# Query and key projections of three head groups by seven products instead of eight, with the output-side query blocks moved and the weight-transform levels rescheduled

## The chip, the cores and the metric

The kernel runs on one core of a Trainium2 chip. The metric is the time of one execution on the device, in microseconds (us). A core has a matrix engine (TensorE, PE in the profile, with its weight loads as PEld), VectorE (DVE), ScalarE (ACT), GpSimd (POOL) and SyncE (SP), which in this kernel only issues DMAs. Each engine takes its instructions in program order and stops at one whose inputs are not ready; everything queued behind it on that engine stops too. The engines wait for each other by semaphores.

## The reference

The input is one sequence `x` of 2048 tokens with 256 features, in float32, and everything is computed in float32. There are two layers, each a layer norm, the layer, another layer norm and the addition to the residual. The first is differential attention, the second a small feed-forward network whose inputs and hidden values pass through a Walsh-Hadamard transform (`fwht`).

```python
x = x + layernorm(attention(layernorm(x)))
x = x + layernorm(ffn(layernorm(x)))

def attention(x):                       # 8 query pairs, 4 key/value groups, D = 128
    q, k, v = split(x @ Wqkv.T + b)     # q: 8 pairs of 2 heads; k: 4 pairs; v: 4 of 256 columns
    p1 = causal_softmax(q[:, 0] @ k[:, 0].T * D ** -0.5)
    p2 = causal_softmax(q[:, 1] @ k[:, 1].T * D ** -0.5)
    o = (p1 - lam * p2) @ v             # 2048 x 256 for each query pair
    o = o * rsqrt(mean(o * o) + eps) * subln_w * (1 - LAMBDA_INIT)
    return concat(o) @ out_w.T + out_b

def ffn(x):                             # 256 -> 1024 -> 256
    x = fwht(x * SU_ug) / 64
    h = silu(x @ W_gate.T * s_gate) * (x @ W_up.T * s_up)
    return (fwht(h * SU_dp) / 64) @ W_down.T * s_down
```

## The kernel before

**Groups and units.** The attention is done for one key/value group `g` (0 to 3) after the other. A group has two query pairs and one key pair, so its projection for 512 tokens (a token block `nb`, 0 to 3) has four parts: the query pairs `j2` = 0 and 1, the key pair `j2` = 2 (256 output columns each, as two heads of 128) and the 256 value columns (part 3). `load_qkv` brings the group's weights `wq`. The attention itself is cut into 96 units, 24 per group. A unit is one tile `i` of 128 tokens, with both of its 64-token halves for `i` below 8 (128 rows here are 64 tokens times two query pairs) and with one half for `i` from 8 on. Group 0 goes through its units with growing `i`; groups 1 to 3 begin with the longest, `i` = 15, and end with `i` = 0. Thus group g begins at unit 24g, the long units of steps 24g to 24g+15 are followed by the short ones, and the last step before a new group has the least attention work.

**Steps.** One loop runs over the steps 0 to 102 and issues, at each, pieces of several units, each piece to the queues of its engines; nothing but this order decides what runs when. The unit of this step gets its scores, the previous one (`mixed`) its combination and its way through DRAM, the one of three steps ago (`ripe`, LAG = 3) its product with the values; `out1` to `out4` are one to four steps older than `ripe`. The order within a step is:

1. the functions in `before[step]`
2. `scores(new, 0)`: TensorE makes scores into PSUM, VectorE moves them to SBUF (`e`) with a row minimum. `exponentials(new, 0)` on ScalarE
3. `inverse(out1)`: GpSimd scales an attention output by its inverse norm. `accumulate(out4)`: VectorE adds an output projection to `acc`. `turn_out(out2)`: VectorE transposes a scaled output, SyncE sends it to DRAM
4. `combine(mixed)`: VectorE forms `p1 - lam * p2`. `move`: VectorE transposes it, SyncE sends it to DRAM (`dr`) and fetches it back as `pt` in four DMAs. For some short units, among them those of groups 1 and 2, the move is issued later, after step 6 of this list
5. the functions in `mid[step]` and then in `between[step]`
6. `pad` (a GpSimd memset), `scores(new, 1)`
7. `values(ripe)`: TensorE multiplies `pt` with the values; ScalarE copies the sum out and takes its squares. `project_out(out3)`: TensorE multiplies with the output weights
8. `exponentials(new, 1)`, then the functions in `after[step]`

`put(where, step, f, ...)` hangs a function into one of the dictionaries `before`, `mid`, `between` and `after`; `put_block` does so for the parts of a token block's projection.

**PSUM.** The pool `ps_s` has three tiles of 128 x 1024, tag `sc`, which scores, all projections and the feed-forward products use in turn; `ps_o` has two tiles for the value products and output projections. A TensorE instruction that is to write a tile waits until the reader of its last contents is done.

**Projections.** `project_heads(g, nb, j2)` makes two heads for 512 tokens: for each head `h` two matmuls of 512 columns (`c` = 0, 1 over the 256 features) into one half of a PSUM tile. A float32 matmul leaves two records in the trace. The first half goes to `qT` or `kT` by a ScalarE activation (L200), the other by a VectorE operation (L202), both with scale (`-SCALE` for queries) and bias. `project_values` makes the values of a block with 8 matmuls of 256 columns. In group 1 the key blocks and block 3's queries are in `before[24]`, the other query blocks in `between` of steps 25 to 30. For groups 2 and 3, beginning at step `end` = 48 and 72, blocks 3, 2 and 1 are in `between` of steps `end`-5 to `end`-1, and block 0 follows, its queries in `between` of `end` and `end`+1.

**Feed-forward weights.** Rather than transform the activations, the kernel transforms the weights. For each of `up`, `gate` and `down`, in a pool `tmp` with two tags `t0` and `t1` of 128 x 2048: `load_weights` (a GpSimd-issued DMA into `t0`, named `raw_...`), for `down` a scaling on ScalarE (`scale_down`), the levels of the transform (`transform(which, n)`, eight GpSimd additions and subtractions of 128 x 256 each, going from one tag to the other; 8 levels for `up` and `gate`, 10 for `down`), `turn_weights` (four VectorE transposes of the result into a tile `x_...` of the tag `t1`, the fourth followed by a SyncE DMA to DRAM, `dw_...`). In before, the levels of `up` are hung into steps 7 to 14, `gate` 18 to 23, `down` 28 to 35, and the pool closes after step 40. From step 74 on the weights are fetched from DRAM (`arrive_weights`).

**The end.** From step 92 on the feed-forward network follows, in pieces between the last units, and after them.

Of the kernel before, what the change touches and what calls it, by code (L numbers as in the profile page):

```python
# [10 lines left out]
F32 = mybir.dt.float32  # L11
BF16 = mybir.dt.bfloat16
AF = mybir.ActivationFunctionType
ALU = mybir.AluOpType
# [35 lines left out]
def kernel(  # L50
# [64 lines left out]
    with ExitStack() as actx:  # L115
# [55 lines left out]
        def project_heads(g, nb, j2, both=True, n=512):  # L171

            wq = loaded[g][0]
            cols4 = ts(nb, n)
            xb, lo = divmod(nb * n, 512)
            nt = n // P
            pp = ps_s.tile([P, 1024], F32, tag="sc", name=f"pp_{g}_{nb}_{j2}_{n}")
            for h in range(2):
                j = 2 * j2 + h
                for c in range(2):  # L180
                    nc.tensor.matmul(  # L181
                        pp[:, 512 * h : 512 * h + n],
                        lhsT=wq[:, c, ts(j, P)],
                        rhs=xnT[:, xb, c, lo : lo + n],
                        start=(c == 0),
                        stop=(c == 1),
                    )
            for h in range(2):
                j = 2 * j2 + h
                col = g * 4 + j if j < 4 else H + g * 2 + j - 4  # L190
                bias = colv[:, C_QKB + col : C_QKB + col + 1]
                src = pp[:, 512 * h : 512 * h + n]
                if j < 4:
                    dst = qT[h][:, ts(nb, nt), :, j2, :].rearrange("d t s q -> d (t s) q")
                    src = src.rearrange("d (t q) -> d t q", q=64)
                else:
                    dst = kT[h][:, cols4]
                scale = -SCALE if j < 4 else 1.0
                if h == 0 or not both:
                    nc.scalar.activation(dst, src, AF.Identity, bias=bias, scale=scale)  # L200
                else:
                    nc.vector.tensor_scalar(dst, src, scale, bias, ALU.mult, ALU.add)  # L202

        def project_values(g, nb):

# [597 lines left out]
        place = {(u.g, u.i, u.subs[0]): k for k, u in enumerate(units)}  # L803


        before, mid, between, after = {}, {}, {}, {}

        def put(where, step, f, *args, **kw):
            where.setdefault(step, []).append(lambda: f(*args, **kw))
# [1 line left out]
        def put_block(where, steps, g, nb, parts, both=True):  # L811
            for step, part in zip(steps, parts):
                if part == 3:
                    put(where, step, project_values, g, nb)
                else:
                    put(where, step, project_heads, g, nb, part, both=both)


        put(before, 0, warm_up)
# [98 lines left out]
        for step in range(len(units) + LAG + 4):  # L918
# [16 lines left out]
                combine(mixed)  # L935
            moved = out2 if complete(out2) else None

            late = mixed and mixed.ns == 2 and (0 < mixed.g < NG - 1 or mixed.g == 0 and mixed.i in (3, 4))
            if not late:
                move(mixed, moved)  # L940
            for f in mid.get(step, ()):
                f()
# [5 lines left out]
            if new:  # L948
                pad(new)
                scores(new, 1)  # L950
            if late:
# [76 lines left out]
```

## Time and profile before

| | |
|---|---|
| median of 3 executions | 1439.21 us (1438.75 to 1439.45) |
| the profiled execution | 1438.5 us, span 1436.7 us, granted TensorE clock 0.999 |
| busy: PE, PEld | 1429.4 (99%), 1042.5 (73%) |
| busy: DVE, ACT, POOL | 976.7 (68%), 503.8 (35%), 362.3 (25%) |
| PE by line | po L376 488.0, sc L268 477.6, pp L181 170.7, pout L443 120.9 |
| POOL, transform L603, all three weights | 163.1 |
| stretch 200 to 400, 400 to 600 | DVE 133.8, 146.2; POOL 68.6, 88.8 |
| stretch 600 to 800, 800 to 1000 | DVE 121.5, 119.5; POOL 24.2, 25.3 |

The span is the time from the first to the last recorded instruction of one profiled execution; the execution takes 1.8 us more than its span. All times within the run are counted from the span's start. "L181" is line 181 of the kernel. The rows give a line, an engine, an operation, the tile it writes and the tile it reads; a count follows an x. The stretches show how VectorE's and GpSimd's work is spread over the run; TensorE is busy for all of each.

### The profile page before, as it was taken

How to read it: one execution, taken by the hardware profiler on the slowest of the kernel's cores; microseconds unless marked ns; L12 is line 12 of the kernel's file. 1: busy time of each engine (PE TensorE's matmuls, PEld its weight loads, DVE VectorE, ACT ScalarE, POOL GpSimd, SP SyncE). 2: the span in 40 equal slices, each digit the busy share in tenths (PEclk: the TensorE clock that was granted, in tenths of full speed). 3: DMA queues.
4: the chain of work that ended last, by engine and by line, in shares of the span. 5: the costliest groups of instructions: out<-in, count | busy, mean ns of one | idle time of the engine just before them, and what ended most of it. 6: DMA issues, size and time to landing. Idle time of an engine off the chain costs nothing.

```text
span 1436.7 us, 16896 instructions
## 1 busy us (share of the span) xinstructions
PE 1429.4 (99%) x5436; PEld 1042.5 (73%) x5436; DVE 976.7 (68%) x1789; ACT 503.8 (35%) x1114; POOL 362.3 (25%) x684
## 2 busy tenths in 40 slices
PE   9999999999999999999999999999999999999998
PEld 7567777656766777776677776676777777888887
DVE  6588787847556777544867678445776788656774
ACT  3453433323133334323433334323424445531111
POOL 2037725830028821011111111111111121121110
PEclk9999999999999999999999999999999999999999
DMA  5379899856667897832798887631999999732110
GB/s 147 74 176 201 190 183 222 175 89 139 154 135 145 166 208 179 165 86 62 156 184 178 172 199 168 129 81 52 208 204 192 193 196 188 173 91 81 52 56 18
DMA packets 501433, 210.76 MB, mean 147 GB/s; under 512 B 396032, under 2 KB 499456, under 8 KB 501216
## 3 DMA queue, kind: packets, MB, share of 16 engines
q1 hardware_dynamic: 498128, 200.73, 66.1%
q0 software_dynamic: 2352, 8.26, 2.1%
q8 instruction: 44, 0.72, 0.2%
q10 hardware_dynamic: 864, 0.68, 0.2%
q14 instruction: 45, 0.37, 0.1%
HBM read 111.05 MB, written 98.57 MB: 146 GB/s over the span
## 4 chain that ended last, share of the span: by engine, by line
PE 99%; DMA 0%; DVE 0%; POOL 0%; issue 0%; ACT 0%; POOLq 0%; DVEq 0%
PE po L376 33%; PE sc L268 32%; PE pp L181 11%; PE gu L706 8%; PE pout L443 8%; PE pd L741 4%; PE pv L210 4%; DMA vb<-in_vbias 0%; PE warm L479 0%; DVE v L217 0%; PE pst L508 0%; ACT q L200 0%; POOL lt L536 0%; DVE stx L90 0%; POOL rsx L95 0%
## 5 line engine op out<-in xcount | busy, mean ns | idle before, releaser
L376 PE MATMUL po<-v,pt 128*128 128x256 f32 x2176 | 488.0, 379 | 0.0
L268 PE MATMUL sc<-k,q 128*128 128x512 f32 (+11 forms) x1280 | 477.6, 519 | 0.3 <-DVE last L281 0.2
L376 PEld LDWEIGHTS po<-v,pt 128*128 128x128 f32 x2176 | 426.5, 196 | 66.5 <-issue 18.3
L268 PEld LDWEIGHTS sc<-k,q 128*128 128x128 f32 x1280 | 240.7, 190 | 200.1 <-issue 156.7
L293 ACT ACTIVATE e<-e,last 128x192 f32<-128x192 f32 (+28 forms) x256 | 298.9, 1169 | 199.4 <-DVE last L281 181.8
L286 DVE TENSOR_SCALAR_CACHE_REDUCE e<-sc 128x1024 f32<-128x1024 f32 (+1 forms) x128 | 149.2, 1166 | 153.3 <-PE sc L268 153.3
L389 ACT COPY osb<-po 128x256 f32<-128x256 f32 (+1 forms) x96 | 42.6, 443 | 483.4 <-PE po L376 482.5
L403 POOL TENSOR_TENSOR u<-ss,ed 128x1 f32<-128x1 f32 (+1 forms) x96 | 20.0, 208 | 750.1 <-ACT po L392 749.9
L325 DVE SCALAR_TENSOR_TENSOR e<-e,cf,e 128x64 f32<-128x64 f32 (+31 forms) x128 | 174.1, 1381 | 3.4
L345 DVE STREAM_TRANSPOSE e<-e 128x1536 f32<-128x1536 f32 (+7 forms) x96 | 166.6, 1735 | 7.1
L181 PE MATMUL pp<-xnT,wq 128*128 128x512 f32 (+1 forms) x408 | 170.7, 568 | 0.1
L281 DVE CUSTOM_DVE_ANT_0 e<-sc,mask 128x64 f32<-128x64 f32 (+15 forms) x128 | 89.2, 718 | 79.9 <-PE sc L268 78.7
L181 PEld LDWEIGHTS pp<-xnT,wq 128*128 128x128 f32 x408 | 77.0, 190 | 79.2 <-issue 76.1
L281 DVE CUSTOM_DVE_ANT_0 e<-sc,mask,mx 128x384 f32<-128x384 f32 (+13 forms) x128 | 105.7, 826 | 23.8 <-PE sc L268 8.4
L443 PE MATMUL pout<-wo,oT 128*128 128x256 f32 x512 | 120.9, 379 | 0.0
L443 PEld LDWEIGHTS pout<-wo,oT 128*128 128x128 f32 x512 | 97.3, 190 | 12.8
L719 ACT ACTIVATE hT<-gu,colv 128x256 f32<-128x256 f32 x64 | 26.8, 470 | 120.9 <-PE gu L706 120.8
L706 PE MATMUL gu<-fxnT,wgate 128*128 128x256 f32 x256 | 65.8, 379 | 0.0
L706 PE MATMUL gu<-fxnT,wup 128*128 128x256 f32 x256 | 65.7, 379 | 0.0
L406 POOL TENSOR_SCALAR osb<-osb,f 128x256 f32<-128x256 f32 x128 | 62.5, 488 | 11.9
L404 POOL TENSOR_TENSOR f<-u,mhalf 128x1 f32<-128x1 f32 (+1 forms) x96 | 58.3, 608 | 7.5
L725 DVE SCALAR_TENSOR_TENSOR hT<-gu,colv,hT 128x256 f32<-128x256 f32 x64 | 30.6, 478 | 41.0 <-ACT hT L719 41.0
(100 smaller groups left out, 1079.5 us busy)
## 6 DMA issues: line engine op xcount, KB each, us to landing
dr<-e SPq DMA_DIRECT2D x20, 1024.0 KB, 4.7
pt<-dr SPq DMA_DIRECT2D x80, 256.0 KB, 5.7
dr<-e SPq DMA_DIRECT2D x20, 896.0 KB, 4.5
pt<-dr SPq DMA_DIRECT2D x80, 224.0 KB, 5.1
do<-xo SPq DMA_DIRECT2D x64, 256.0 KB, 3.8
oT<-do SPq DMA_DIRECT2D x256, 64.0 KB, 2.6
dr<-e SPq DMA_DIRECT2D x20, 768.0 KB, 4.3
pt<-dr SPq DMA_DIRECT2D x80, 192.0 KB, 4.5
```

The source lines that it names most:

```text
L181: nc.tensor.matmul(pp[:, 512 * h : 512 * h + n], lhsT=wq[:, c, ts(j, P)], rhs=xnT[:, xb, c, lo : lo + n], start=(c == 0), stop=(c == 1),)
L268: nc.tensor.matmul(src[:, k, :], lhsT=qT[m][:, u.i, u.subs[a]].rearrange("d p q -> d (p q)"), rhs=kT[m][:, lo : lo + w // n], start=True, ...
L281: nc.vector.tensor_tensor_reduce(dst, src, msk, 1.0, best, ALU.add, ALU.min, accum_out=u.last[:, k0 : k0 + 1])
L286: nc.vector.tensor_scalar(dst, src, 1.0, best, ALU.mult, ALU.min, accum_out=least)
L293: nc.scalar.activation(e, e, AF.Exp, bias=u.last[:, 2 * a + m : 2 * a + m + 1], scale=-1.0, accum_out=u.d[:, a, m : m + 1],)
L325: nc.vector.scalar_tensor_tensor(e0, e1, cf[:, a : a + 1], e0, ALU.mult, ALU.add)
L345: nc.vector.transpose(x[:, : 256 * ng].rearrange("p (g c r) -> p r g c", g=ng, r=2), e[:, : 256 * ng].rearrange(order, g=ng, r=2),)
L376: nc.tensor.matmul(u.po[:, ts(a, HID)], lhsT=ptv[:, g, r, :], rhs=vt[:, kc, :], start=(kc == 0), stop=(kc == u.i),)
L404: nc.gpsimd.tensor_tensor(f[:, : u.ns], w[:, : u.ns], mhalf[:, : u.ns], ALU.pow)
L406: nc.gpsimd.tensor_scalar(u.osb[:, a, :], u.osb[:, a, :], f[:, a : a + 1], 16.0, ALU.mult, ALU.mult)
L443: nc.tensor.matmul(u.pout[:, :HID], lhsT=u.oT[:, c, p, :], rhs=wos[u.g][:, p, c, :], start=(p == 0 and c == 0), stop=(p == 1 and c == 1),)
L706: nc.tensor.matmul(ps[:, ts(2 * j + n, 256)], lhsT=ffn[which][:, c, ts(fc, P)], rhs=xnT[:, c, :], start=(c == 0), stop=(c == 1),)
```

## The change

It has three parts, all in the attention phase.

**Seven products.** For the groups 1 to 3 `project_heads` is replaced by `project_fast`. The block is seen as a product of 2 x 2 blocks: the weights as two heads by two feature halves, the tokens as two feature halves by two runs of 256 tokens. By Strassen's scheme in Winograd's form seven matmuls of 256 columns take the place of eight (four of 512), spread over two PSUM tiles: four products in the first, three in the second. Sums of weights are made once for each group and head pair (`weight_sums`), sums of tokens once for each group and token block (`token_sums`), on GpSimd. The query weights are scaled by `-SCALE` beforehand (`scale_queries`, on ScalarE). The results are put together by two ScalarE copies, five VectorE operations and two GpSimd additions. The buffers come from a new pool `fast`, opened after step `end`-7 and closed after step `end`+6 in group 1 and `end`+2 in the others.

**Another place.** The late query blocks (group 1's blocks 0 to 2, block 0 of the groups 2 and 3) go from `between` to a new dictionary `late`, whose functions are called after `project_out` and before `exponentials(new, 1)`.

**The transforms.** `down` now comes first (load after step 30, levels after 31 to 37), then `up` (load after 50, levels after 51 to 54, two in each step), then `gate` (load after 57, levels after 58 to 61, two in each). The pool `fold` is opened for `down`, closed after step 40, opened again for `up` and `gate` and closed after step 64.

```diff
+        def scale_queries(g):
+            wq = loaded[g][0]
+            for c in range(2):
+                nc.scalar.activation(wq[:, c, :512], wq[:, c, :512], AF.Copy, scale=-SCALE)
+
+        def weight_sums(g, j2):
...
+            nc.gpsimd.tensor_tensor(s1, a21, a22, ALU.add)
+            nc.gpsimd.tensor_tensor(s2, s1, a11, ALU.subtract)
+            nc.gpsimd.tensor_tensor(s3, a11, a21, ALU.subtract)
+            nc.gpsimd.tensor_tensor(s4, a12, s2, ALU.subtract)
...
+        def token_sums(g, nb):
...
+            nc.gpsimd.tensor_tensor(t1, b12, b11, ALU.subtract)
+            nc.gpsimd.tensor_tensor(t2, b22, t1, ALU.subtract)
+            nc.gpsimd.tensor_tensor(t3, b22, b12, ALU.subtract)
+            nc.gpsimd.tensor_tensor(t4, b21, t2, ALU.subtract)
...
+        def project_fast(g, nb, j2):
...
+            for k, todo in enumerate(
+                (
+                    ((a11, b11), (sw[:, 1, :], tw[:, 1, :]), (a12, b21), (sw[:, 2, :], tw[:, 2, :])),
+                    ((sw[:, 0, :], tw[:, 0, :]), (sw[:, 3, :], b22), (a22, tw[:, 3, :])),
+                )
+            ):
+                pp = ps_s.tile([P, 1024], F32, tag="sc", name=f"pf_{n}_{k}")
+                for at, (w, t) in enumerate(todo):
+                    nc.tensor.matmul(pp[:, ts(at, 256)], lhsT=w, rhs=t, start=True, stop=True)
+                tiles.append(pp)
...
+            p1, p6, p2, p7 = (pa[:, ts(k, 256)] for k in range(4))
+            p5, p3, p4 = (pb[:, ts(k, 256)] for k in range(3))
...
+            nc.scalar.copy(m1, p1)
+            nc.scalar.copy(m5, p5)
+            nc.vector.tensor_tensor(u, p6, m1, ALU.add)
+            nc.vector.scalar_tensor_tensor(
+                place(0, 0), split(p2), bias0, split(m1), ALU.add, ALU.add
+            )
+            nc.vector.scalar_tensor_tensor(w, p7, bias1, u, ALU.add, ALU.add)
+            nc.vector.tensor_tensor(place(1, 0), split(p4), split(w), ALU.add)
+            nc.vector.scalar_tensor_tensor(
+                place(0, 1), split(p3), bias0, split(u), ALU.add, ALU.add
+            )
+            nc.gpsimd.tensor_tensor(place(1, 1), split(w), split(m5), ALU.add)
+            nc.gpsimd.tensor_tensor(place(0, 1), place(0, 1), split(m5), ALU.add)
...
-                    put(where, step, project_heads, g, nb, part, both=both)
+                    put(where, step, project_fast, g, nb, part)
...
+            put(after, end - 7, open_fast, g)
+            put(after, end - 7, scale_queries, g)
+            for j2 in range(3):
+                put(after, end - 7 + j2 // 2, weight_sums, g, j2)
             if g == 1:
 
+                put(after, end - 3, token_sums, g, 3)
+                put(after, end - 3, token_sums, g, 0)
+                put(after, end - 2, token_sums, g, 1)
+                put_block(before, [end] * 3, g, 3, [0, 1, 2])
+                put(before, end, token_sums, g, 2)
                 for nb in range(3):
-                    put_block(between, [end + 5 - 2 * nb, end + 6 - 2 * nb], g, nb, [0, 1])
-                put_block(before, [end] * 2, g, 3, [0, 1])
+                    put_block(before, [end], g, nb, [2])
+                    put_block(late, [end + 5 - 2 * nb, end + 6 - 2 * nb], g, nb, [0, 1])
                 for nb in range(4):
-                    put_block(before, [end], g, nb, [2])
                     put_block(after, [end + 2], g, nb, [3])
+                put(after, end + 6, close_fast)
             else:
+                for step, nb in ((end - 7, 3), (end - 6, 2), (end - 5, 1), (end - 3, 0)):
+                    put(after, step, token_sums, g, nb)
...
-                put_block(between, [end, end + 1], g, 0, [0, 1])
+                put_block(late, [end, end + 1], g, 0, [0, 1])
                 put_block(after, [end + 2], g, 0, [3])
+                put(after, end + 2, close_fast)
...
-        put(after, 5, open_fold)
-        for which, begin_at, steps in (
-            ("up", 5, range(7, 15)),
-            ("gate", 17, (18, 19, 20, 21, 22, 22, 23, 23)),
-            ("down", 26, (28, 29, 29, 30, 30, 31, 32, 33, 34, 35)),
+        for which, begin_at, steps, end in (
+            ("down", 30, (31, 32, 33, 33, 34, 35, 35, 36, 36, 37), 40),
+            ("up", 50, (51, 51, 52, 52, 53, 53, 54, 54), 0),
+            ("gate", 57, (58, 58, 59, 59, 60, 60, 61, 61), 64),
         ):
+            if which != "gate":
+                put(after, begin_at, open_fold)
             put(after, begin_at, load_weights, which)
...
-        put(after, 40, lambda: ffn["tmp_stack"].close())
+            if end:
+                put(after, end, lambda: ffn["tmp_stack"].close())
...
             if complete(out3):
                 project_out(out3)
+            for f in late.get(step, ()):
+                f()
             if new:
                 exponentials(new, 1)
```

`turn_weights` follows each transform as before: part 0 after the step behind the last level, parts 1 and 2 in `mid` and `after` of the next, part 3 in `mid` of the one after.

More of the change, by code (lines that the diff above doesn't have):

```diff
@@ L202, in project_heads, with open_fast, close_fast @@
                     nc.vector.tensor_scalar(dst, src, scale, bias, ALU.mult, ALU.add)
+        fast = {}
+        def open_fast(g):
+            fast["stack"] = ExitStack()
+            fast["pool"] = fast["stack"].enter_context(
+                tc.tile_pool(name="fast", bufs=1, side="right")
+            )
+            fast["t"], fast["s"] = {}, {}
+        def close_fast():
+            fast["stack"].close()
+        def scale_queries(g):
+            wq = loaded[g][0]
+            for c in range(2):
+                nc.scalar.activation(wq[:, c, :512], wq[:, c, :512], AF.Copy, scale=-SCALE)
@@ new lines, in weight_sums @@
+        def weight_sums(g, j2):
+            wq = loaded[g][0]
+            sw = fast["pool"].tile([P, 4, P], F32, tag=f"sw{j2}", name=f"sw_{g}_{j2}")
+            a11, a12, a21, a22 = (wq[:, c, ts(2 * j2 + h, P)] for h in range(2) for c in range(2))
+            s1, s2, s3, s4 = (sw[:, k, :] for k in range(4))
+            nc.gpsimd.tensor_tensor(s1, a21, a22, ALU.add)
+            nc.gpsimd.tensor_tensor(s2, s1, a11, ALU.subtract)
+            nc.gpsimd.tensor_tensor(s3, a11, a21, ALU.subtract)
+            nc.gpsimd.tensor_tensor(s4, a12, s2, ALU.subtract)
+            fast["s"][j2] = sw
@@ new lines, in token_sums @@
+        def token_sums(g, nb):
+            tw = fast["pool"].tile([P, 4, 256], F32, tag="tw", name=f"tw_{g}_{nb}_{len(fast['t'])}", bufs=3)
+            b11, b12, b21, b22 = (xnT[:, nb, c, ts(k, 256)] for c in range(2) for k in range(2))
+            t1, t2, t3, t4 = (tw[:, k, :] for k in range(4))
+            nc.gpsimd.tensor_tensor(t1, b12, b11, ALU.subtract)
+            nc.gpsimd.tensor_tensor(t2, b22, t1, ALU.subtract)
+            nc.gpsimd.tensor_tensor(t3, b22, b12, ALU.subtract)
+            nc.gpsimd.tensor_tensor(t4, b21, t2, ALU.subtract)
+            fast["t"][nb] = tw
@@ new lines, in project_fast, with split, place @@
+        def project_fast(g, nb, j2):
+            wq = loaded[g][0]
+            sw, tw = fast["s"][j2], fast["t"][nb]
+            a11, a12, a21, a22 = (wq[:, c, ts(2 * j2 + h, P)] for h in range(2) for c in range(2))
+            b11, b12, b21, b22 = (xnT[:, nb, c, ts(k, 256)] for c in range(2) for k in range(2))
+            n = f"{g}_{nb}_{j2}"
+            tiles = []
+            for k, todo in enumerate(
[8 more added lines that the diff above has]
+                tiles.append(pp)
+            pa, pb = tiles
+            p1, p6, p2, p7 = (pa[:, ts(k, 256)] for k in range(4))
+            p5, p3, p4 = (pb[:, ts(k, 256)] for k in range(3))
+            y = fast["pool"].tile([P, 4, 256], F32, tag="y", name=f"yf_{n}", bufs=2)
+            m1, u, w, m5 = (y[:, k, :] for k in range(4))
+            col = g * 4 + 2 * j2 if j2 < 2 else H + g * 2
+            bias0, bias1 = (colv[:, C_QKB + col + h : C_QKB + col + h + 1] for h in range(2))
+            def split(v):
+                return v.rearrange("d (t q) -> d t q", q=64) if j2 < 2 else v
+            def place(h, k):
+                if j2 == 2:
+                    return kT[h][:, 512 * nb + 256 * k : 512 * nb + 256 * (k + 1)]
+                t0 = 4 * nb + 2 * k
+                return qT[h][:, t0 : t0 + 2, :, j2, :].rearrange("d t s q -> d (t s) q")
+            nc.scalar.copy(m1, p1)
[8 more added lines that the diff above has]
+                place(0, 1), split(p3), bias0, split(u), ALU.add, ALU.add
+            )
+            nc.gpsimd.tensor_tensor(place(1, 1), split(w), split(m5), ALU.add)
+            nc.gpsimd.tensor_tensor(place(0, 1), place(0, 1), split(m5), ALU.add)
@@ L803 @@
         place = {(u.g, u.i, u.subs[0]): k for k, u in enumerate(units)}
-        before, mid, between, after = {}, {}, {}, {}
+        before, mid, between, late, after = {}, {}, {}, {}, {}
         def put(where, step, f, *args, **kw):
@@ L936 @@
             moved = out2 if complete(out2) else None
-            late = mixed and mixed.ns == 2 and (0 < mixed.g < NG - 1 or mixed.g == 0 and mixed.i in (3, 4))
-            if not late:
+            behind = mixed and mixed.ns == 2 and (0 < mixed.g < NG - 1 or mixed.g == 0 and mixed.i in (3, 4))
+            if not behind:
                 move(mixed, moved)
@@ L950 @@
                 scores(new, 1)
-            if late:
+            if behind:
                 move(mixed, moved)
```

## The prediction

> **What bounds the kernel now.** I read the page first (busy shares, the chain that ended last), then the chain in order of time, then the timelines of single engines where the change works. Times are microseconds from the span's start. "Step" is the place in the list of units; group g begins at step 24g.
>
> ```profile
> PE 1429.4 (99%) x5436; PEld 1042.5 (73%) x5436; DVE 976.7 (68%) x1789; ACT 503.8 (35%) x1114; POOL 362.3 (25%) x684
> ...
> PE 99%; DMA 0%; DVE 0%; POOL 0%; issue 0%; ACT 0%; POOLq 0%; DVEq 0%
> ```
>
> TensorE is never waiting outside the first 15 us and the tail: whatever it no longer does is gained, and each new wait of it is lost in full. The chain in order of time gives the pitch of its instructions (each fp32 matmul leaves two records):
>
> ```profile
> 298.34 20.60 PE pp L181 x48
> ...
> 367.57 13.81 PE pv L210 x64
> ```
>
> 48 records of 512 columns in 20.60 us are 0.429 us each, 64 records of 256 columns in 13.81 us are 0.216.
>
> **The matmuls removed and added.** A block of `project_heads` is 4 matmuls of 512 columns, 8 records, 3.43 us. A block of `project_fast` is 7 matmuls of 256 columns, 14 records, 3.02 us. Three groups times four token blocks times three head pairs are 36 blocks: 36 x 0.41 = **14.8 us less**. The pv row has another weight for every 256 columns too, so the pitch holds.
>
> **What VectorE, ScalarE and GpSimd get.** Per block one ACT activation (0.69) and one DVE operation (0.74 to 0.75) go. In come two ACT copies (0.37, as osb<-po 128x256), five DVE operations (two like acc<-pout 0.42, three like hT<-gu 0.48: 2.28 in all) and two POOL additions. DVE gains 36 x 1.53 = 55 us, to some 72% of the span: not a bound by its sum, so what counts is how late it hands back PSUM. The scores and projections share three PSUM tiles, and a fast block takes two of them. In the built program the first copy waits for all four products of its tile, the second for all three of the other. From the end of the four: 0.2 (the gap between PE's end and its reader in every row), copy 0.37, then u, q/k and w, 0.42 + 0.48 + 0.48: the tile is free 2.0 us after its last product, if DVE is free. PE meanwhile does the other three products (1.30) and the first score tile of half 1; for the second score tile it needs this tile back.
>
> [...]
>
> Step 43 (group 2's first block, between the score halves of unit i=4) is the worst place, since DVE comes late to it:
>
> ```profile
> 576.70 2.05 DVE L345 STREAM_TRANSPOSE e<-e 128x1792 f32<-128x1792 f32 x1
> ...
> 580.71 1.88 DVE L325 SCALAR_TENSOR_TENSOR e<-e,cf,e 128x704 f32<-128x704 f32 x2
> ```
>
> DVE is free at 582.6, frees the tile at 582.6 + 1.38 = 584.0; PE, which would have the block done at 581.9 and the first score tile at 583.0, wants it then: a wait of 1.1. The same walk gives 0.6 in step 44 (two blocks: 0.4 at the second block's second tile, 0.2 at the scores), 0.1 in step 45, 0.3 in step 46, 0.55 in step 47, and 0.3 where the late block meets the long units' evictions in step 49. That is 3.0 us for group 2, the same for group 3 (steps 67 to 73): **+6.0** (0 to 10: 0 if DVE's order gives the tiles back sooner, 10 if POOL slows DVE as in the row of 2.72 for an e<-e,cf,e of 1984 columns beside POOL's transform, against 2.29 without).
>
> Group 1's six blocks stand one behind the other in step 24; DVE needs 2.3 of each 3.02, so nothing stalls until the last key block: its last half goes pb end + 0.2 + 0.37 + 0.42 + 0.48, then POOL's addition 0.8, then PE: 2.6 after the products, where the scores that need it start 1.7 after: **+0.9** (0 to 2). The late query blocks of steps 25 to 30 sit behind 7 us of values with DVE idle: 0. Scaling wq (six ACT instructions of about 0.7), weight and token sums (36 and 48 POOL operations, in steps 17 to 24, 41 to 46, 65 to 70, where POOL is idle but for about 1.5 us per step) are covered; if token sums came late, PE would wait for them, up to 1 us in steps 43 and 67.
>
> **The moved transform levels.** This part decides. The 208 POOL operations stay, but the order is now down, up, gate, and gate runs two levels per step in steps 58 to 61, where a step of PE takes 10 us. In before the same gate chain shows its start:
>
> ```profile
> 216.18 0.67 DVE L622 STREAM_TRANSPOSE x_up<-t_up 128x512 f32<-128x512 f32 x1
> ```
>
> ```profile
> 220.62 7.15 SPq L360 DMA_DIRECT2D pt<-dr  x4
> 227.95 1.05 SPq L625 DMA_DIRECT2D dw_up<-x_up  x1
> ```
>
> ```profile
> 234.61 6.32 POOL L603 TENSOR_TENSOR t_gate<-raw_gate 128x256 f32<-128x256 f32 x8 [13.60 <-DMA dw_up<-x_up]
> ...
> 242.38 4.61 POOL L603 TENSOR_TENSOR t_gate<-t_gate 128x256 f32<-128x256 f32 x8
> ...
> 248.62 7.32 POOL L603 TENSOR_TENSOR t_gate<-t_gate 128x256 f32<-128x256 f32 x8
> ```
>
> The first level writes the tile that x_up leaves, so it waits until dw_up has landed; dw_up is issued by SP behind four pt<-dr issues, which took 7.15 while raw_gate was loading (2.0 elsewhere). From the end of the last x_up transpose (216.85) to the first level are 17.8 us. In after, that transpose stands in step 57 (794.9 to 795.5 on before's clock), and up, gate's order on SP and POOL is the same: first level at **813.3**. Then 64 operations at 0.784 (the mean of all 208: 163.1 us), 50.2, and between them three steps' `inverse`, pad and vb issue, 5.3: **868.8**. Who waits: DVE, in order, behind `turn_out` of step 62 (it needs the `inverse` that is queued behind six levels) and then the first transpose of t_gate at the end of step 62, and behind that the evictions of step 63. While DVE stands still POOL runs at 0.58 (the 4.61 row, where DVE was mostly idle); some 14 us of that give back 4: 864.8. PE's need:
>
> ```profile
> 849.56 4.04 PE L268 MATMUL sc<-k,q 128*128 128x512 f32 x12
> 853.44 4.49 PE L376 MATMUL po<-v,pt 128*128 128x256 f32 x20
> ```
>
> In step 63 the last score tile (128 columns) is due at 853.2 and needs the tile of step 63's first eviction: transpose 0.67, eviction 1.2, gap 0.1 after the transform ends. PE waits 864.8 + 2.0 - 853.2 = **+13.6**. Bounds: 0, if the level starts when raw_gate lands (issue to landing 10.6: 806.2) and all run at 0.58 (848.4); 26, if all run at 0.92 (the 7.32 row: 877.4). I take the middle because POOL's means in the three transforms (0.77 to 0.81) come from steps in which DVE was as busy as here. In before the same lag was harmless: gate had one level per step at first, and steps of 11 to 15 us.
>
> [...]
>
> Up (steps 51 to 54, steps of 12 to 15 us) fits: 4 x 13 us of POOL, ending at 766 where DVE wants it at 773: 0. Down now starts when the fast pool closes: load at 451, landing 461.6, scaling to 464, 61.7 + 9 of POOL: 535, wanted by 537.6: **+0.5** (0 to 4).
>
> **Sum.** -14.8 + 6.0 + 0.9 + 13.6 + 0.5 = +6.2. The profiled execution took 1438.5 (span 1436.7 and 1.8 around it); with it 1444.7. The median of the runs shown lies 0.7 higher: **1445.4**.
>
> **Rivals.** (1) Gate fits: POOL is ready by 851, no wait of DVE for t_gate. For it: POOL's 4.61 row, and that raw_gate lands 7 us before dw_up does. Against it: the 13.60 wait in the row above, and 64 operations in 38 us would need the uncontended pace throughout. Then -14.8 + 7.4: 1438.5 - 7.4 + 0.7 = 1431.8, faster. The point from which it decides: a transform end 7 us earlier than 864.8 brings the change to about zero, 13.6 earlier to this. Chance 0.24. (2) In between (end at 854 to 861): 1436 to 1442, chance 0.13. (3) Worse: contended pace, or DVE's lag carried into steps 64 to 67, where group 3's weight sums must wait for dw_gate: +6 more, 1451, chance 0.10. (4) The products don't save: were each 256-column record to cost half of 512's 592 ns duration rather than the pitch, seven would take longer than four; the pitch rows say no: 0.02. My forecast: 0.51, its own range 1442 to 1450.
>
> **Numbers.** A measurement of this kernel can tell about 0.2% (2.9 us) from no change. Slower by more: 0.51 + 0.10 + 0.02 = 0.63; faster by more: 0.24; within: 0.13. The range leaves out half of the worst cases and the faster half of rival 1: 1431 to 1450.
>
> **What would show it.** PE's busy time lower by about 14 us but the span longer; in the waits, DVE's transpose of t_gate waiting some 5 to 8 us for POOL, and `turn_out` of step 62 some 7 us; PE idle in one place of some 14 us near step 63, and pieces of 0.1 to 1.1 us in steps 43 to 47 and 67 to 71, released by DVE. Wrong if POOL ends gate before DVE asks (no such wait), or if the waits in the block steps are absent or several times as long.

## The result and the profile after

The changed kernel takes **1449.09 us** (median of 4, 1447.83 to 1449.24) against 1438.98 us before (median of 4): a ratio of 1.0068, 95% interval 1.0051 to 1.0086. It is slower by 10.1 us, forecast 1445.4 in a range of 1431 to 1450. The profiled execution has a span of 1447.4 us, 10.7 more than before.

The page of the kernel after: the busy shares, TensorE's busy tenths in 40 slices, its granted clock in tenths, and the chain that ended last.

```profile
PE 1422.6 (98%) x5652; PEld 1084.2 (75%) x5652; DVE 1019.8 (70%) x1933; ACT 509.8 (35%) x1156; POOL 467.1 (32%) x840
...
PE   9999999999999999999999969999999999999998
...
PEclk9999999999999999999999989999999999999999
...
PE 90%; POOL 5%; DVE 3%; issue 1%; DMA 1%; SPq 0%; ACT 0%; POOLq 0%; DVEq 0%; ACTq 0%
```

TensorE does less work (1422.6 instead of 1429.4 busy) in a longer span, and the chain now has other engines in it: 10% of it is no longer TensorE. One slice in 40 stands out, the 24th (832 to 868 us), with TensorE at 6 tenths and its clock below full. TensorE's waits after (engine and line, what was waited for, total us, times, longest) say for whom:

```profile
PE sc L357 <- DVE e L375: 12.3, 4, 7.1
PE sc L357 <- DVE yf L285: 4.0, 4, 1.7
...
PE sc L357 <- POOL k L291: 0.5, 1, 0.5
```

To see where the 10.7 us arise, one can use that both kernels make the same 1280 records of score matmuls in the same order. The start of the first one of each step, after minus before, is a running ledger of gains (negative) and losses, which ends at the +10.7 of the spans:

| steps | work | ledger, from and to | change | predicted |
|---|---|---|---|---|
| 23 to 31 | group 1: 12 fast blocks | 0.0 to -4.2 | -4.2 | -4.9 + 0.9 = -4.0 |
| 32 to 43 | down's transform | -4.2 to -4.2 | 0.0 | +0.5 |
| 43 to 50 | group 2: 12 fast blocks | -4.2 to -5.6 | -1.4 | -4.9 + 3.0 = -1.9 |
| 51 to 57 | up's transform | -5.5 to -3.9 | +1.6 | 0 |
| 62 to 64 | gate's transform | -3.9 to +12.0 | +15.9 | +13.6 |
| 67 to 74 | group 3: 12 fast blocks | +12.0 to +10.6 | -1.4 | -1.9 |

The loss stands almost whole in one place, step 63: step 64 begins at 859.49 us in the kernel before and at 871.46 in the kernel after. The timelines there, engine by engine (start, us, line, operation, and in brackets the idle time before it and what ended it). First SyncE and GpSimd, from gate's first level on:

```profile
797.17 4.33 SPq L449 DMA_DIRECT2D pt<-dr  x4
801.61 1.10 SPq L714 DMA_DIRECT2D dw_up<-x_up  x1
```

```profile
808.52 5.95 POOL L692 TENSOR_TENSOR t_gate<-raw_gate 128x256 f32<-128x256 f32 x8 [12.05 <-DMA dw_up<-x_up]
...
849.23 12.34 POOL L692 TENSOR_TENSOR t_gate<-t_gate 128x256 f32<-128x256 f32 x16
```

The last level ends at 861.6. VectorE, in order, met the late GpSimd three times (a pad, the scaled output of step 62 and the transform):

```profile
836.05 1.51 DVE L434 STREAM_TRANSPOSE e<-e 128x1280 f32<-128x1280 f32 x1 [3.55 <-POOL e L401]
...
849.19 0.71 DVE L508 STREAM_TRANSPOSE xo<-osb 128x512 f32<-128x512 f32 x1 [7.95 <-POOL osb L495]
...
861.61 0.71 DVE L711 STREAM_TRANSPOSE x_gate<-t_gate 128x512 f32<-128x512 f32 x1 [5.83 <-POOL t_gate L692]
862.25 1.19 DVE L375 TENSOR_SCALAR_CACHE_REDUCE e<-sc 128x1024 f32<-128x1024 f32 x1
```

and TensorE, which needs the score tiles that VectorE holds, stood still twice:

```profile
846.07 1.88 PE L357 MATMUL sc<-k,q 128*128 128x512 f32 x4
855.07 4.55 PE L357 MATMUL sc<-k,q 128*128 128x128 f32 x6 [7.12 <-DVE e L375]
863.50 0.80 PE L357 MATMUL sc<-k,q 128*128 128x128 f32 x2 [3.88 <-DVE e L375]
```

The stretches around it (busy us of PE, PEld, DVE, ACT, POOL, then the granted clock, which is the share of TensorE's full speed, DMA share and GB/s) show a second thing: after the idle time TensorE works at half clock, 0.51 in 855 to 860 and again in 863.3 to 866.8.

```profile
855.00:860.00 5.00, 4.55 (x6) 1.67 (x6) 0.64 (x3) 1.39 (x3) 4.92 (x8) 0.51 0.86 233
860.00:863.30 3.30, 0.00 (x0) 0.00 (x0) 1.69 (x2) 0.00 (x0) 3.07 (x8) 1.00 0.97 124
863.30:866.80 3.50, 3.30 (x9) 2.76 (x10) 3.18 (x8) 1.35 (x2) 1.37 (x4) 0.51 0.00 0
```

The smaller loss, up's, was not forecast. GpSimd after, steps 53 to 55, and VectorE at the end of step 55:

```profile
745.67 0.83 POOL L154 DMA_DIRECT2D wo<-in_outwT  x1 [13.91 <-PE pout L532]
746.53 13.21 POOL L692 TENSOR_TENSOR t_up<-t_up 128x256 f32<-128x256 f32 x16
```

```profile
774.16 0.71 DVE L711 STREAM_TRANSPOSE x_up<-t_up 128x512 f32<-128x512 f32 x1 [4.67 <-POOL t_up L692]
```

The load of group 2's output weights stands ahead of four levels of up in GpSimd's queue, and it may not write its tile before TensorE's last `project_out` of group 1 has read it: GpSimd stood for 13.9 us. VectorE then waited for up, and TensorE for VectorE.

### The profile page after: what moved, and what is told of

It reads as the page before. It is cut to its first block, busy times and chain, and to the rows that moved or that the text cites. A ratio compares the mean times of both kernels' runs of the same rounds, so it can differ in the third digit from the quotient of the medians.

```text
span 1447.4 us, 17822 instructions
## 1 busy us (share of the span) xinstructions
PE 1422.6 (98%) x5652; PEld 1084.2 (75%) x5652; DVE 1019.8 (70%) x1933; ACT 509.8 (35%) x1156; POOL 467.1 (32%) x840
## 4 chain that ended last, share of the span: by engine, by line
PE 90%; POOL 5%; DVE 3%; issue 1%; DMA 1%; SPq 0%; ACT 0%; POOLq 0%; DVEq 0%; ACTq 0%
PE po L465 29%; PE sc L357 28%; PE gu L795 8%; PE pout L532 7%; PE pf L260 7%; PE pd L830 4%; PE pv L299 4%; POOL t_gate L692 3%; PE pp L181 2%; POOL t_up L692 1%; DVE e L414 1%; DMA dw_up<-x_up 0%; DMA vb<-in_vbias 0%; DVE e L370 0%; PE warm L568 0%
## 5 line engine op out<-in xcount | busy, mean ns | idle before, releaser
L465 PEld LDWEIGHTS po<-v,pt 128*128 128x128 f32 x2176 | 427.5, 197 | 66.8 <-issue 18.2
L414 DVE SCALAR_TENSOR_TENSOR e<-e,cf,e 128x64 f32<-128x64 f32 (+31 forms) x128 | 173.3, 1374 | 3.4
L290 POOL TENSOR_TENSOR q<-yf 128x256 f32<-128x256 f32 x24 | 17.7, 739 | 195.2 <-DVE yf L285 164.4
L495 POOL TENSOR_SCALAR osb<-osb,f 128x256 f32<-128x256 f32 x128 | 64.5, 504 | 11.9
L493 POOL TENSOR_TENSOR f<-u,mhalf 128x1 f32<-128x1 f32 (+1 forms) x96 | 61.6, 642 | 7.5
L260 PE MATMUL pf<-tw,sw 128*128 128x256 f32 x216 | 59.2, 381 | 0.2
```

The lines of the kernel that those rows point to most:

```text
L260: nc.tensor.matmul(pp[:, ts(at, 256)], lhsT=w, rhs=t, start=True, stop=True)
L414: nc.vector.scalar_tensor_tensor(e0, e1, cf[:, a : a + 1], e0, ALU.mult, ALU.add)
L465: nc.tensor.matmul(u.po[:, ts(a, HID)], lhsT=ptv[:, g, r, :], rhs=vt[:, kc, :], start=(kc == 0), stop=(kc == u.i),)
L493: nc.gpsimd.tensor_tensor(f[:, : u.ns], w[:, : u.ns], mhalf[:, : u.ns], ALU.pow)
L495: nc.gpsimd.tensor_scalar(u.osb[:, a, :], u.osb[:, a, :], f[:, a : a + 1], 16.0, ALU.mult, ALU.mult)
```

## The experiments

The theory is that the whole loss is the schedule's: the two transforms end after VectorE asks for them, and the seven products would by themselves be a gain. The rival is that the loss comes of what the products put on VectorE, ScalarE and GpSimd.

**1. The schedule alone.** The kernel before, with the changed order of the transforms and nothing else.

```diff
...
-            ("up", 5, range(7, 15)),
-            ("gate", 17, (18, 19, 20, 21, 22, 22, 23, 23)),
-            ("down", 26, (28, 29, 29, 30, 30, 31, 32, 33, 34, 35)),
+            ("down", 30, (31, 32, 33, 33, 34, 35, 35, 36, 36, 37), 40),
+            ("up", 50, (51, 51, 52, 52, 53, 53, 54, 54), 0),
+            ("gate", 57, (58, 58, 59, 59, 60, 60, 61, 61), 64),
...
```

> The kernel before, with nothing of the change but the new schedule of the weight transforms (down after 30, up after 50, gate after 57 with two levels per step); all projections stay as before. Theory S (the loss is the schedule's: GpSimd ends the transforms after VectorE asks for them, whatever the projections are): TensorE loses in steps 56 to 58 the 1.6 us and in steps 62 to 64 the 15.9 us that it loses in the changed kernel, so 1439.0 + 17.5 = 1456.5 us (1453 to 1459), with one half-clock stretch near step 64. Rival P (the loss comes of the new load of VectorE, ScalarE and GpSimd by the seven products): no such stall, 1439 us (1438 to 1441).

Measured 1457.84 us, 1.0133 of before (1.0118 to 1.0148). The ledger against before rises by 0.5 us in step 39, where `down` is turned, by 1.5 in steps 55 to 57 and by 15.6 in steps 62 to 64 (+2.6 to +18.2). TensorE's waits of this run (lines as in the kernel before):

```profile
PE sc L268 <- DVE e L286: 12.0, 3, 7.1
```

Both stalls, `up`'s and `gate`'s, are there within 0.3 us of their size in the changed kernel, with no fast block in the program. The rival falls.

**2. The schedule undone**, all else as in the change.

```diff
+            ("up", 5, range(7, 15), 17),
...
-            ("up", 50, (51, 51, 52, 52, 53, 53, 54, 54), 0),
-            ("gate", 57, (58, 58, 59, 59, 60, 60, 61, 61), 64),
+            ("gate", 50, range(51, 59), 64),
...
```

> The changed kernel, with up's transform back in steps 5 to 17 as before and gate's in steps 50 to 61, one level per step; down as in the change. Theory S: both stalls (1.6 and 15.9 us) are gone, and what is left is the gain of the projections, 4.2 us in steps 24 to 30, 1.4 to 1.8 in steps 43 to 49 and 1.3 to 1.8 in steps 67 to 73: 1439.0 - 7.4 = 1431.6 us (1430 to 1433), granted clock back at 0.999. Rival P: the stalls near step 63 stay or move, over 1440 us.

Measured 1432.70 us, 0.9958 (0.9943 to 0.9973): faster than before by 6.0. Its waits:

```profile
PE sc L357 <- DVE yf L285: 4.0, 4, 1.7
...
PE pout L532 <- DMA oT<-do: 0.7, 1, 0.7
```

Both stalls are gone. The ledger shows 4.2 us gained in group 1 and 1.4 in each of the others (between the steps of the table above), and 0.9 lost in step 63, where an output projection waits for its transposed tile.

**3. A tile of its own for the turned weights.** Gate's first level writes the tile that x_up leaves, and so waits for dw_up.

```diff
-                ffn["turned"] = ffn["tmp"].tile([P, 2 * INTER], F32, tag="t1", name=f"x_{which}")
+                ffn["turned"] = ffn["tmp"].tile([P, 2 * INTER], F32, tag="t2", name=f"x_{which}")
```

> The changed kernel, but the turned weights (x_up, x_gate, x_down) get a tile of their own instead of taking turns with the levels' second tile. Theory Q (gate starts late because its first level waits until dw_up, queued on SyncE behind four pt fetches, has read the tile): the first level starts when raw_gate has landed, near 803 instead of 808.5 us; everything of the stall moves 5.5 us ahead, so 1443.6 us (1442 to 1445). Rival R (GpSimd's pace alone decides; the start is bound by something else, such as the load itself landing at 808): no change, 1449 us.

Measured 1439.36 us, 1.0002 (0.9992 to 1.0011). GpSimd's row of the first level:

```profile
799.64 5.84 POOL L692 TENSOR_TENSOR t_gate<-raw_gate 128x256 f32<-128x256 f32 x8 [4.58 <-DMA raw_gate<-in_wgate]
```

That is 4 us below the expected time: gate gained more than forecast, and up's loss went too. The start does follow raw_gate's landing, but the load was issued 1.2 us earlier than in the change and took 8.5 us instead of 9.6 (10.6 in the trace before), so the first level came 8.9 us earlier rather than 5.5. The ledger's loss in steps 62 to 64 fell by as much, from 15.9 to 7.0. For up, x_up was turned at 771.7 instead of 774.2. GpSimd did not get through up's last level any sooner (774.4 against 774.1), so here the first transpose began 2.7 us before the end of that level. In the program it reads only half of the level's results, but in the shared tile it overwrites what all of the level reads, so there it waits for the end.

**4. The load of wo behind the levels.**

```diff
-            put(after, end + LAG + 2, load_wo, g)
+            put(before, end + LAG + 3, load_wo, g)
```

> The changed kernel, but the load of the output weights of group 2, issued by GpSimd, stands behind the two levels of up in step 53 instead of ahead of them. Theory W (GpSimd stood still for 13.9 us before that load, because its target is read by TensorE's last output projection of group 1, and with it four levels of up): up ends some 13 us earlier, VectorE's wait of 4.7 us for x_up and TensorE's loss of 1.6 us in steps 56 to 58 are gone, gate stays: 1447.5 us (1446.8 to 1448.3). Rival R (two levels per step are too many for steps of 14 us): no change, 1449 us.

Measured 1447.19 us, 1.0058 (1.0043 to 1.0073). The load now finds its tile nearly free, and the ledger holds -5.6 from step 50 to 63; gate's loss (16.0) is untouched.

```profile
745.52 0.83 POOL L154 DMA_DIRECT2D wo<-in_outwT  x1 [0.96 <-PE pout L532]
```

**5. The wait filled**, to price the half clock.

```diff
+                    again = 1
+                    if (u.g, u.i, u.subs[0], c) == (2, 8, 1, 0):
+                        again = 3 if half else 5
-                    for k in range(n):
+                    for k in list(range(n)) * again:
```

> The changed kernel, but in step 63 TensorE repeats the matmuls of the first score tile of half 0 five times and those of half 1 three times (the same values into the same tile), so that it works through most of its two waits for VectorE. Theory C (behind the waits TensorE ran at half clock for 3.4 us, and that cost some 1.7 us after the second wait, besides the refilling of its pipeline): no half-clock stretch near step 64, the same wait for the transform, and 1449.1 - 2 = 1447 us (1446.3 to 1447.8). Rival N (the clock cost nothing that the wait did not hide): 1449 us. Should the repeats hold up the chain themselves, over 1450 us.

Measured 1446.80 us, 1.0050 (1.0035 to 1.0065), 2.3 us less than the change by the medians; in the ledger the loss of steps 62 to 64 is 14.2 us instead of 15.9. TensorE's rows:

```profile
846.54 8.75 PE L360 MATMUL sc<-k,q 128*128 128x512 f32 x20
...
863.97 0.49 PE L360 MATMUL sc<-k,q 128*128 128x128 f32 x2 [2.26 <-DVE e L378]
...
870.35 6.82 PE L360 MATMUL sc<-k,q 128*128 128x480 f32 x16
```

The last tile of step 63 comes no earlier than in the change, but from there to the next step's scores are 6.4 us instead of 8.0 (863.50 to 871.46), and the span's clock is 0.999 instead of 0.996. The half clock cost 1.6 to 1.7 us behind the stall; its first stretch cost nothing, as it lay between two waits.

**6. The early schedule in the kernel before**, to see whether it gains by itself. The edit is that of experiment 2, in the kernel before.

> The kernel before with the transform schedule of the run with the schedule undone (up in 5 to 17, down in 30 to 40, gate one level per step in 50 to 61), all projections as before. Theory S (a schedule that ends in time moves nothing else): 1438.7 to 1439.8 us, with the 0.9 us of step 63 that a wait for oT behind dw_gate cost in that run. Then that run's gain of 6.0 us is the projections' alone. Rival: the new places free something by themselves, under 1437 us.

Measured 1440.52 us, 1.0006 (0.9997 to 1.0015). The ledger stays within 0.1 us of before up to step 63 and loses 1.6 there, more than forecast. So the gain of run 2 is the projections'.

**7. All blocks late.** On run 2: the blocks of steps 43 to 47 and 67 to 71 behind `project_out`.

```diff
-                put_block(between, [end - 5, end - 4, end - 4, end - 3], g, 3, range(4))
-                put_block(between, [end - 3, end - 3, end - 2, end - 2], g, 2, range(4))
-                put_block(between, [end - 2, end - 1, end - 1], g, 1, range(3))
+                put_block(late, [end - 5, end - 4, end - 4, end - 3], g, 3, range(4))
+                put_block(late, [end - 3, end - 3, end - 2, end - 2], g, 2, range(4))
+                put_block(late, [end - 2, end - 1, end - 1], g, 1, range(3))
```

> The run with the schedule undone (1432.7 us), with all blocks of groups 2 and 3 that stood between the score halves of steps 43 to 47 and 67 to 71 put behind project_out as well. Theory D (the waits there, 3.5 us per group, come of VectorE reaching the block late, behind the transpose of a short unit or its combination): behind the value products VectorE has caught up, most of the waits go: 1432.7 - 5 = 1427.7 us (1426 to 1429.5). Rival T (a block takes two of three tiles for 2 us whatever VectorE does before; the waits only move to the next step's scores): 1432.7 us (1431.5 to 1434).

Measured 1432.38 us, 0.9949 (0.9933 to 0.9966): not to be told from run 2. Where two or three blocks end a step, their tiles are missing at the next step's scores, as at the start of step 47:

```profile
642.52 0.41 PE L357 MATMUL sc<-k,q 128*128 128x64 f32 x2 [0.39 <-DVE yf L285]
643.45 0.68 PE L357 MATMUL sc<-k,q 128*128 128x128 f32 x4 [0.52 <-DVE last L370]
```

Step 43's wait fell from 1.7 to 0.1, and others came in its place: theory T.

**8. No block late.** On run 2: the late query blocks back between the score halves.

```diff
-                    put_block(late, [end + 5 - 2 * nb, end + 6 - 2 * nb], g, nb, [0, 1])
+                    put_block(between, [end + 5 - 2 * nb, end + 6 - 2 * nb], g, nb, [0, 1])
...
-                put_block(late, [end, end + 1], g, 0, [0, 1])
+                put_block(between, [end, end + 1], g, 0, [0, 1])
```

> The run with the schedule undone, with the late query blocks (steps 25 to 30, 48 and 49, 72 and 73) put back between the score halves, where they stood before the change. Theory D: in the long units VectorE comes to the block behind a combination and a transpose, and TensorE waits 0.3 to 1 us for a tile in each of the ten steps: 1432.7 + 5 = 1437.7 us (1435 to 1441). Rival: VectorE has time enough in steps of 14 us and the place is worth nothing: 1432.7 us.

Measured 1473.78 us, 1.0236 (1.0221 to 1.0251), some 41 us above run 2: right in its sign, eight times too small in its size. TensorE's waits, and step 29 on VectorE and TensorE:

```profile
PE sc L357 <- DVE yf L285: 30.5, 13, 4.5
```

```profile
438.54 2.02 DVE L414 SCALAR_TENSOR_TENSOR e<-e,cf,e 128x1728 f32<-128x1728 f32 x1
440.66 2.04 DVE L434 STREAM_TRANSPOSE e<-e 128x1792 f32<-128x1792 f32 x1
...
443.32 0.47 DVE L285 SCALAR_TENSOR_TENSOR yf<-pf,colv,yf 128x256 f32<-128x256 f32 x1
```

```profile
439.88 1.88 PE L357 MATMUL sc<-k,q 128*128 128x512 f32 x4
443.94 1.75 PE L357 MATMUL sc<-k,q 128*128 128x384 f32 x4 [2.18 <-DVE yf L285]
```

The block's products end at 439.9, but VectorE comes to them only behind 4 us of combination and transpose. A stretch of half clock (0.52) stands behind this wait:

```profile
445.00:448.50 3.50, 3.50 (x10) 2.55 (x9) 1.88 (x4) 0.00 (x0) 0.52 (x1) 0.52 0.49 155
```

The waits for this line went from 4.0 to 30.5 us. The rest of the 41 us, some 15, fits the half clock, as an estimate: the profiled execution's granted clock is 0.989 against 0.999 in run 2, and that hundredth of its 1473.5 us is 14.7.

**9 to 12. The remaining waits.** Run 9 is run 2 with only the first block of groups 2 and 3 late and gate's levels a step earlier:

```diff
-                put_block(between, [end - 5, end - 4, end - 4, end - 3], g, 3, range(4))
+                put_block(late, [end - 5], g, 3, [0])
+                put_block(between, [end - 4, end - 4, end - 3], g, 3, range(1, 4))
...
+            ("gate", 50, (51, 51, 52, 53, 54, 55, 56, 57), 64),
```

> The run with the schedule undone (1432.7 us), with two edits: of groups 2 and 3 only the first block (steps 43 and 67) goes behind project_out, and gate's levels stand a step earlier, so that dw_gate is issued after step 60. Theory D' (between the score halves only the first block costs much, 1.8 us per group, as VectorE comes to it from a long combination; behind project_out it cost 0.3; the others cost 0.3 to 0.4 in either place, and up to 1.1 where two stand behind project_out): 3.0 us for both groups, and 0.9 for the wait for oT behind dw_gate in step 63: 1428.8 us (1427.8 to 1430). Rival (a block moved alone pushes its wait to step 44's blocks): 1431.5 to 1433 us.

Measured 1432.10 us, 0.9949 (0.9935 to 0.9963), the rival's number. The wait of step 43 is gone, and a wait stands in front of the second block of step 44 instead:

```profile
PE pf L260 <- DVE yf L285: 2.0, 2, 1.0
```

Step 63 still loses 1.2 us with dw_gate issued earlier. SyncE's queue in this run shows how: dw_gate now stands directly ahead of the load of group 3's weights.

```profile
830.51 0.90 SPq L714 DMA_DIRECT2D dw_gate<-x_gate  x1
831.45 4.60 SPq L145 DMA_DIRECT2D wq<-in_wqkv  x4
```

The four issues of wq took 4.60 us, against 2.84 in the kernel before. The store of a transposed tile (`dr`) behind them was issued 2.9 us later than in the kernel before (with the ledger's 5.6 us taken off), and the fetch of the output projection's tile for step 63 was still 1.9 us later. So dw_gate seems to delay this queue in either place, here by way of wq. No run was made with the two far apart.

Run 10 is run 9, with ScalarE and GpSimd making a piece of the query blocks in VectorE's place:

```diff
-            nc.vector.scalar_tensor_tensor(
-                place(0, 0), split(p2), bias0, split(m1), ALU.add, ALU.add
-            )
+            if j2 == 2:
+                nc.vector.scalar_tensor_tensor(
+                    place(0, 0), split(p2), bias0, split(m1), ALU.add, ALU.add
+                )
+            else:
+                nc.scalar.activation(place(0, 0), split(p2), AF.Identity, bias=bias0)
+                nc.gpsimd.tensor_tensor(place(0, 0), place(0, 0), split(m1), ALU.add)
```

> The same as the run beside it, but in the query blocks the piece P1 + P2 + bias is made by ScalarE (P2 + bias) and GpSimd (+ P1) instead of VectorE. Theory V (the first tile is held by three VectorE operations; with two it comes free 0.5 us sooner): the remaining waits of some 1.6 us per group go down by half, 1427.5 us (1426.5 to 1428.8). Rival G (GpSimd's third addition, or ScalarE's second copy, comes late for the scores that read the queries, in step 24 above all): the same or slower, 1428.8 to 1432 us.

Measured 1438.56 us, 0.9996 (0.9987 to 1.0005), slower than both forecasts: the gain is lost. ScalarE's read of the tile waited for VectorE's, and VectorE's next one for it:

```profile
596.95 0.47 ACT L287 ACTIVATE q<-pf,colv 128x256 f32<-128x256 f32 x1 [1.43 <-DVE yf L281]
```

```profile
597.46 0.48 DVE L289 SCALAR_TENSOR_TENSOR yf<-pf,colv,yf 128x256 f32<-128x256 f32 x1 [0.54 <-ACT q L287]
```

Run 11 is run 10, but ScalarE's instruction stands directly behind its first copy, so that the tile changes hands once:

```diff
             nc.scalar.copy(m1, p1)
+            if j2 < 2:
+                nc.scalar.activation(place(0, 0), split(p2), AF.Identity, bias=bias0)
             nc.scalar.copy(m5, p5)
...
-                nc.scalar.activation(place(0, 0), split(p2), AF.Identity, bias=bias0)
```

> The run with one block late (1432.1 us), with the piece P2 + bias of the query blocks made by ScalarE directly behind its copy of P1, and P1 added by GpSimd; in the last run ScalarE's instruction stood behind its copy of P5, and in the trace it waited for VectorE's u, and VectorE's w for it. Theory O (it was that handing back and forth that held the tile, and the loss of 6 us; in order, the tile is held for two ScalarE and two VectorE operations): 1431 to 1432.5 us. Rival G (GpSimd's third addition or ScalarE's work comes late whatever the order): 1435 us or more.

Measured 1432.37 us, 0.9954 (0.9942 to 0.9967): back to run 9's time. It was the handing over, not the third GpSimd addition. Run 12 is run 9 with step 44's and 68's second block late as well:

```diff
-                put_block(between, [end - 4, end - 4, end - 3], g, 3, range(1, 4))
+                put_block(between, [end - 4, end - 3], g, 3, [1, 3])
+                put_block(late, [end - 4], g, 3, [2])
```

> The run with one block late (1432.1 us), with the second of the two blocks of steps 44 and 68 behind project_out as well. In that run the wait left was 1.2 us in front of this block's second tile. Theory D'' (a block costs a wait where it follows another block or a long combination within 3 us; alone behind project_out it costs 0.3): 2 x 0.9 us less, 1430.3 us (1429.5 to 1431.3). Rival (the waits are handed on once more): 1431.6 to 1432.6 us.

Measured 1435.34 us, 0.9975 (0.9965 to 0.9984): worse than run 9 and than both forecasts. The wait of 1.0 us became one of 1.9, now for the scores of half 1 in step 44, as the one block left between the halves is followed by scores at once. The waits of a short unit's step can be pushed about, but no place was found that takes them away. The best versions (runs 2, 7, 9, 11: 1432.1 to 1432.7) can't be told apart; run 9 beats before by 7.4 us.

## Why the prediction was right, and where its terms were off

**The sum.** The measured 1449.09 us lie 3.7 above the forecast and 0.9 below the end of the range. By the ledger the terms missed by +2.3 (gate), +1.6 (up), +1.1 (waits of groups 2 and 3), -0.5 (down) and -0.2 (group 1), mostly one way. That the sum came so close owes something to luck: gate's 13.6 was a middle chosen between 0 and 26.

**The products.** Right: group 1 came to -4.2, with one wait of 0.5 us for GpSimd's last key piece (0.7 in the ledger) where 0.9 was forecast. The terms listed for that wait add up to 2.3 us behind the products, not to the 2.6 stated, which would have made it 0.6.

**PSUM waits of groups 2 and 3.** +6.0 forecast, 7.1 measured (the 2 x 4.93 of the products less the 2.8 gained). The walk named the place and cause, but step 43 cost 1.9 (a wait of 1.7, and 0.2 more in the ledger) and not 1.1, and the other steps of a group 1.6 together and not 1.9. VectorE after:

```profile
577.11 2.24 DVE L414 SCALAR_TENSOR_TENSOR e<-e,cf,e 128x704 f32<-128x704 f32 x2
...
580.00 0.47 DVE L285 SCALAR_TENSOR_TENSOR yf<-pf,colv,yf 128x256 f32<-128x256 f32 x1
```

The combination began later and took 2.24 instead of the 1.88 of the trace before, and the tile came back at 580.5, which is 584.7 on the clock of before, where 584.0 was forecast. Whether these waits would shrink if the first copy did not wait for all four products of its tile, no run tried.

**Up: the step that failed.** The prediction said that up fits, counting 4 x 13 us of GpSimd. It did not count what up's levels are moved behind in that queue: `load_wo` after step 53, a DMA issue that waits for TensorE. The 13.9 us of standing still and the 1.6 us of loss are shown by the rows above and by run 4.

**Gate.** The mechanism was right in its parts: the first level was forecast at 813.3 on the clock of before and came at 808.5 + 3.9 = 812.4; the end at 864.8 and came at 865.5; VectorE's waits of 7 and 5 to 8 us were 7.95 and 5.83. Run 3 shows that the start decides, run 1 that nothing of the products is in it. What the forecast lacked is the clock: of the 2.3 us missing, 0.7 is the later end and 1.6 the half clock of run 5. The half clock is also the larger part of why TensorE's busy time fell by 6.8 us and not by the 14 forecast (in run 2, without it, it fell by 11.9), and the idle time lay in two pieces (7.1 and 3.9), not in one.

One reading under this term was wrong, though little came of it. The prediction took 0.58 us for an operation as GpSimd's pace while VectorE stands still, from a row of 4.61 us for eight (its "uncontended" pace; the slowest it used, 0.92, is from a row of 7.32). But 4.61 is what the transform's first two levels take when no combination falls into them, with VectorE busy too; the later levels take 5.5 at the least, in the trace before and in the one after. Two levels of the kernel after, the first beside a busy VectorE, the second with VectorE idle throughout:

```profile
703.66 4.61 POOL L692 TENSOR_TENSOR t_up<-raw_up 128x256 f32<-128x256 f32 x8 [3.07 <-DMA raw_up<-in_wup]
```

```profile
842.25 5.51 POOL L692 TENSOR_TENSOR t_gate<-t_gate 128x256 f32<-128x256 f32 x8
```

So the lower bound with all operations at 0.58 could not be reached: two levels at 4.6 and six at 5.5 are 42 us and not 37. Gate's 64 operations took 47.7 us, where 50.2 - 4 were forecast; they began 0.9 earlier and ended 0.7 later.

**Down** cost nothing in the change (0.5 forecast), and 0.5 in run 1.

**The late blocks.** Their value was named only as a zero cost in the prediction. Run 8 shows that this zero is what the change lives on: the cover of the value products is worth 41 us.

## What to carry to other kernels

Cutting TensorE's instructions is worth only what the engines behind it hand back in time: 14.8 us of matmuls became 6 to 7 us, since a fast block holds two of three PSUM tiles until VectorE comes to it, and where such a block is placed mattered more (41 us) than what it saved. When work is moved along an in-order queue, list everything it is moved behind, DMA issues with their waits too, and where a chain must end by a given time look at what holds its start: a buffer shared with the last chain's store cost 9 us here. A stall of the main engine can cost more than its length, by the clock that follows it: 1.6 us here behind the wait of 3.9 us in step 63, and by the estimate some 15 us in run 8.

## What the runs showed of the hardware

**The clock.** In the kernel after, TensorE's granted clock was 0.50 for 6.8 us, from 853.1 to 859.9, at the end of and behind the wait of 7.12 us; it was 1.00 in the 3.4 us after that, and 0.50 again for 3.4 us, from 863.3 to 866.8, from the end of the wait of 3.88 us on. In run 8 it was 0.50 from 445.1 to 448.5, behind the wait of 2.18 us. Not every wait of this length had such a stretch behind it: the wait of 2.26 us in run 5 had none (1.00 up to 866.1, and 0.999 for the span), and run 12, with waits of up to 1.9 us, has 0.999 for its span, as the kernel before. TensorE was busy for 1.23 us of the 3.41 that hold run 8's wait; run 5's wait lies in two stretches of that length, with 2.44 and 2.13 us of work. Run 8's with the one behind it, then run 5's two (length, then the columns as above, PE's busy time first):

```profile
441.71:445.12 3.41, 1.23 (x5) 0.81 (x5) 3.31 (x7) 0.00 (x0) 1.07 (x2) 1.00 0.42 144
445.12:448.53 3.41, 3.41 (x10) 2.46 (x9) 1.76 (x4) 0.00 (x0) 0.40 (x1) 0.50 0.48 149
```

```profile
859.27:862.69 3.42, 2.44 (x6) 0.76 (x4) 0.61 (x1) 0.00 (x0) 3.34 (x7) 1.00 1.16 188
862.69:866.10 3.41, 2.13 (x11) 1.98 (x12) 3.19 (x8) 1.35 (x2) 2.29 (x7) 1.00 0.08 8
```

What decides whether half clock follows a wait, these runs do not show.

**GpSimd beside VectorE's combination.** In the kernel after, the 185 transform operations that lay beside no combination (L414) took some 0.61 us in the first two levels and 0.72 to 0.73 in the later ones, beside a transpose, an eviction or an idle VectorE alike, and at most 0.9. But one that began 0.4 us or more into a combination waited it out: in all 11 such cases of the kernel after it ended 0.47 to 0.59 us after the combination. In step 60:

```profile
822.83 2.11 POOL L692 TENSOR_TENSOR t_gate<-t_gate 128x256 f32<-128x256 f32 x1
```

```profile
822.23 2.12 DVE L414 SCALAR_TENSOR_TENSOR e<-e,cf,e 128x1408 f32<-128x1408 f32 x1
```

Of the 208 transform operations after, the 23 that lay mainly beside L414 took 1.39 us in the mean, the others 0.70. So here the transform's time went by the level and by how many combinations fell into it (the later level with none, the row of 842.25, took 5.51 us), not by whether VectorE was busy, as the prediction had it.
